# Products with values taken from a queue by pairs of heads in the last attention loop, with other TensorE work in every second round

## The chip, the cores and the metric

The kernel runs on one core of one Trainium2 chip. The metric is the time of the whole kernel on the device, in microseconds; each version is run several times and the median counts. Beside the times there is one profiled execution, whose instructions, waits and transfers can be looked up one by one. TensorE (PE) multiplies matrices, VectorE (DVE) and ScalarE (ACT) work element by element, GpSimd (POOL) does small work and issues stores, and SyncE (SP) issues loads.

## The reference, cut to what matters

Two layers work on 4 images of 64 x 64 positions with 128 channels, so 4096 tokens each. Layer 0 is a selective scan in three directions. Layer 1 is attention with 16 heads of width 8, in which one tensor serves as query, key and value, followed by a small feed-forward part, and then by 64 experts of which each takes its 8 best tokens of an image. What the change touches is the attention of the last image:

```python
qkv = _qz_ring(heads + rx_theta)
q = jnp.transpose(qkv, (0, 2, 1, 3))
scores = jnp.einsum('bhsd,bhtd->bhst', q, q) / np.sqrt(D)
attn = jax.nn.softmax(scores, axis=-1)
ctx = jnp.einsum('bhst,bhtd->bhsd', attn, q)
```

and the gathering of the experts' inputs, which is done on TensorE, with matrices that are zero except at the chosen tokens:

```python
gathered = jnp.take_along_axis(x, flat_idx[:, :, None], axis=1)
pooled = jnp.einsum('bked,bke->bed', gathered, topv)
```

## The kernel before, in words

Attention runs image by image in `loop` (line 948). The loops of the first three images lie beside the scans of the image that follows. This document is about the fourth and last loop, which has no scan left to go with it.

A loop has 1024 **rounds**. A round is one group j of four heads, one block qb of 512 queries and one tile kc of 128 keys; 32 rounds with kc from 0 to 31 make a **turn**. In the last loop the turns are sorted by query block (`by_block`), so that one block of 512 tokens after the other becomes complete, every 128 rounds. A round needs

- `scores` (988): four matmuls on TensorE, two into each of two tiles `s` (PSUM, three of them in rotation), each on a quarter of the array's rows; then two exponentials on ScalarE, each from a tile `s` of 128 x 1024 into a tile `e` (SBUF, pool `a_exps`, four in rotation);
- `values` (1006): four matmuls on TensorE, one for each head of the group, each from half a tile `e` with 32 columns of weights into 32 partitions of the accumulator `acc`. The four lie on four quarters of the array's columns. Heads 0 and 1 read the first tile `e` of the round (pair 0), heads 2 and 3 the second (pair 1).

Within the loop each engine carries out its instructions in the order in which the code issues them: the scheduler is switched to manual. In round i the body of the loop (1040 to 1054) issues the scores of round i + 1, then a share of **other work** (`beside`, 1051), then the values of round i. After a turn `sums` (1018) copies the accumulator to `av` (on VectorE in the last loop), and three rounds later `store` sends `av` to DRAM with five DMAs that GpSimd issues.

The other work of the last loop is a chain of generators, held by `Pace` (1494). Each `yield` ends a step. A step that begins with a matmul is announced by `yield PE`, either by `bank.take` or by `pause` (861), which cuts a group of matmuls in two. `Pace.turn` (1510) adds 1.5 steps of credit in each round and carries out steps while there is credit; a step with a matmul only where the round is `free`, and only one of them in a round. The call at line 1619 says which rounds are free:

```python
block.loop(nb - 1, lambda i: last.turn(1.5, i % 3 > 0 or i > 830), True)
last.rest()
```

So two rounds of three are free up to round 830, and all of them after it. What is not done when the loop ends is carried out by `last.rest()` (1620), before the work that follows. In the chain stand, in this order: `after` for all eight blocks of the third image (context times `w_comb`, norms and the feed-forward part: `first` with matmuls `co`, `second` with matmuls `zt`, `h`, `fo`, `xT`, `lg`), the experts' biases, the search and choice of tokens and the gathering (`pool`, 1333, with four matmuls `wt` and four matmuls `pool` for each of 24 pieces) of images 0 to 2, and then `after` for blocks 0 to 3, 4 to 5 and 6 of the fourth image itself, each of which has to wait until attention has completed its blocks, and one more search. All of these share one PSUM bank (`Bank(…, 1)`), so that a step which wants it waits for the step that has it.

Behind the loop come `closing` (1629), which is `after` for block 7 of the fourth image, the choice and the gathering for that image, the experts, and the scatter of their answers. Weights for three groups of experts are fetched at an early step of `closing` (1632), into memory that the loop has given back.

Of the kernel before, what the change touches and what calls it, by code (L numbers as in the profile page):

```python
# [11 lines left out]
F32 = mybir.dt.float32  # L12
# [4 lines left out]
P = 128  # L17
C = 128
L = 4096
NT = L // P  # L20
# [14 lines left out]
QB = 512  # L35
# [51 lines left out]
PE = "pe"  # L87
# [626 lines left out]
class Attention:  # L714
# [62 lines left out]
    def begin(self, loop):  # L777

        tc = self.tc
        self.pieces_of(loop, 2)  # L780
        self.big = loop.enter_context(tc.tile_pool(name="a_big", bufs=1))
        self.mid = loop.enter_context(tc.tile_pool(name="a_mid", bufs=2))
        self.exps = loop.enter_context(tc.tile_pool(name="a_exps", bufs=4))
        self.ps_s = loop.enter_context(tc.tile_pool(name="a_ps_s", bufs=3, space=PSUM))
        self.ps_o = loop.enter_context(tc.tile_pool(name="a_ps_o", bufs=1, space=PSUM))

# [161 lines left out]
    def loop(self, b, beside, by_block=False):  # L948


        nc = self.nc
        self.cut = by_block
        self.context[b] = self.dram.tile([P, L], F32, name=f"d_ctx_{b}")
        self.total[b] = self.dram.tile([L // QB, H, QB], F32, name=f"d_sum_{b}")
        self.whole[b] = 0
        turns = [(j, qb) for j in range(4) for qb in range(L // QB)]
        if by_block:
            turns.sort(key=lambda turn: turn[1])
        rounds = [(j, qb, kc) for j, qb in turns for kc in range(NT)]
        queries, keys, weights, es, accs, later = {}, {}, {}, {}, {}, {}  # L960
        chunks = [(j, g) for j, _ in turns for g in range(NT // 4)]
        held = {}

        def halves(to, j, cut, first):


            src = self.q[b].rearrange("(k j) x d t -> j k (x d) t", j=4)[j]
            nc.sync.dma_start(out=to, in_=src[:, first * D : (first + 4) * D, cut])

        def fetch(at):  # L970

            if at >= len(chunks):
                return
            j, g = chunks[at]
            if held.get(g) != j:
                held[g] = j
                keys[g] = self.big.tile([P, QB], F32, tag="keys", bufs=10, name=f"key_{b}_{at}")
                halves(keys[g], j, slice(g * QB, (g + 1) * QB), 0)
                weights[g] = self.big.tile([P, 4, VJ], F32, tag="values", bufs=10, name=f"val_{b}_{at}")
                nc.sync.dma_start(out=weights[g], in_=self.v[b][:, j, g * 4 : g * 4 + 4, :])  # L980
            keys[f"{at}"], weights[f"{at}"] = keys[g], weights[g]

        def masked(j, qb):
            t = self.mid.tile([P, QB], F32, tag="qm", name=f"qm_{b}_{j}_{qb}")
            halves(t, j, slice(qb * QB, (qb + 1) * QB), 2)
            queries[j, qb] = t

        def scores(i):

            j, qb, kc = rounds[i]  # L990
            es[i] = []
            cut = slice(kc % 4 * P, kc % 4 * P + P)
            for pair in range(2):
                s_ps = self.ps_s.tile([P, 2, QB], F32, tag="s", name=f"s_{b}_{i}_{pair}")
                for k in range(2):
                    at = 32 * (2 * pair + k)
                    rows = slice(at, at + 32)
                    nc.tensor.matmul(  # L998
                        s_ps[:, k, :], keys[f"{i // 4}"][rows, cut].bitcast(F32R), queries[j, qb][rows, :].bitcast(F32R),
                        start=True, stop=True,  # L1000
                    )
                e = self.exps.tile([P, 2, QB], F32, tag="e", name=f"e_{b}_{i}_{pair}")
                nc.scalar.activation(e, s_ps, AF.Exp, scale=1.0 / math.sqrt(D))  # L1003
                es[i].append(e)

        def values(i):
            j, qb, kc = rounds[i]
            if kc == 0:
                accs[j, qb] = self.ps_o.tile([P, QB], F32, tag="acc", name=f"acc_{b}_{j}_{qb}")
            v = weights[f"{i // 4}"][:, kc % 4, :]  # L1010
            for k in range(4):
                nc.tensor.matmul(  # L1012
                    accs[j, qb][32 * k : 32 * k + 32, :], v[:, k * VW : k * VW + 32],
                    es[i][k // 2][:, k % 2, :], start=(kc == 0), stop=(kc == NT - 1),
                )
            del es[i]

        def sums(j, qb, i):

            av = self.mid.tile([P, QB], F32, tag="av", name=f"av_{b}_{j}_{qb}")  # L1020
            (nc.vector.tensor_copy if by_block else nc.scalar.copy)(av, accs.pop((j, qb)))  # L1021
            cut = slice(qb * QB, (qb + 1) * QB)

            def store():
                for k in range(4):
                    h = 4 * k + j
                    nc.gpsimd.dma_start(  # L1027
                        out=self.context[b][h * D : h * D + D, cut], in_=av[32 * k : 32 * k + D, :]
                    )
                nc.gpsimd.dma_start(  # L1030
                    out=self.total[b][qb].rearrange("(k j) t -> j k t", j=4)[j], in_=av[D::32, :]
                )
                if by_block and j == 3:
                    self.whole[b] = qb + 1

            later[i + 3] = store

        masked(0, 0)
        for at in range(3):
            fetch(at)  # L1040
        scores(0)
        for i, (j, qb, kc) in enumerate(rounds):
            if i % 4 == 0:
                fetch(i // 4 + 3)
            if i + 1 < len(rounds):
                scores(i + 1)
            if kc == NT - 12 and i + 12 < len(rounds):
                masked(*rounds[i + 12][:2])
            if i in later:
                later.pop(i)()  # L1050
            beside(i)
            values(i)
            if kc == NT - 1:
                sums(j, qb, i)
        for i in sorted(later):
            later[i]()
        self.whole[b] = L // QB
# [181 lines left out]
class Experts:  # L1239
# [93 lines left out]
    def pool(self, b, g):  # L1333

        nc, bank, rows = self.nc, self.block.bank, slice(b % 2 * E, b % 2 * E + E)
        x = self.some.tile([P, 4, C], F32, tag="x", bufs=4, name=f"x_{b}_{g}")
        nc.sync.dma_start(out=x, in_=self.block.xn[b][:, g * 4 : g * 4 + 4, :])
        yield
        ps = yield from bank.take(f"wt_{b}_{g}")
        for i in range(4):  # L1340
            at = (g * 4 + i) * P
            nc.tensor.matmul(
                ps[:, i * E : (i + 1) * E], self.chosen[b // 2][rows, at : at + P], self.diagonal[rows, b // 2, :],
                start=True, stop=True,
            )
        yield
        wT = self.some.tile([P, 4, E], F32, tag="wT", name=f"wT_{b}_{g}")
        nc.vector.tensor_copy(wT.rearrange("p i e -> p (i e)"), ps[:, : 4 * E])
        bank.leave()
        yield  # L1350
        ps = yield from bank.take(f"pool_{b}_{g}")
        for i in range(4):
            nc.tensor.matmul(ps[:, :E], x[:, i, :], wT[:, i, :], start=(i == 0), stop=(i == 3))
        yield
        into = self.pooled[:, :, b]
        if g == 0:
            nc.vector.tensor_copy(into, ps[:, :E])
        else:
            nc.vector.tensor_add(into, into, ps[:, :E])
        bank.leave()  # L1360
        yield
# [132 lines left out]
class Pace:  # L1494
# [15 lines left out]
    def turn(self, share, free):  # L1510

        self.credit = min(self.credit + share, 3.0)
        while self.credit >= 1 and not self.done and (free or self.then is not PE):
            free = free and self.then is not PE
            self.step()

    def rest(self):
        while not self.done:
# [3 lines left out]
def tile_kernel(tc, ctx, x, in_proj_w, dirs, out_proj_w, attn, gate, weight1, weight2, out):  # L1522
# [3 lines left out]
    nb = x.shape[0]  # L1526
# [42 lines left out]
    loop = ExitStack()  # L1569
# [39 lines left out]
    with tc.manual_schedule():  # L1609
        last = Pace(  # L1610
            last.parts, experts.biases(),
            *(
                part for images in pairs[:-1]
                for part in (experts.search(images, blocks), experts.choice(images, blocks), experts.gather(images))
            ),
            block.after(nb - 1, range(0, 4)), block.after(nb - 1, range(4, 6)), block.after(nb - 1, range(6, blocks - 1)),
            experts.search(pairs[-1], blocks - 1),
        )
        block.loop(nb - 1, lambda i: last.turn(1.5, i % 3 > 0 or i > 830), True)
        last.rest()  # L1620
        block.cut = False
    loop.close()
# [49 lines left out]
```

## Time and profile before

| what | us |
|---|---|
| median of 3 runs | 11400.93 |
| lowest and highest run | 11396.92, 11414.34 |
| the profiled execution, its own time | 11412.32 |
| the span of its instructions | 11410.5 |
| first exponential of the last loop starts | 9126.4 |
| last product with values of the last loop starts | 11160.8 |
| exponentials in the last loop | 2048 |
| mean granted clock of TensorE over the span | 0.942 |

The profiled execution took 1.8 us more than its span, and 11.4 us more than the median. Times within it are counted from the start of the span. The last loop therefore takes up about 2034 us of it, and what follows about 250 us.

How to read it: the page of a profile gives the busy time of each engine, the busy share in 40 slices of equal length, the chain of work that ended last, and the costliest groups of instructions by line with the mean duration of one and the idle time before them. A timeline lists instructions in order of time and merges equal ones. A table of stretches gives the busy time of each engine between two times, with the granted clock of TensorE.

### The profile page before, as it was taken

The page shows a single profiled execution, that of the slowest core. Times are in us where ns is not written, and L with a number is a line of the kernel's source. Part 1 is how long each engine was busy: PE and PEld are TensorE (multiplying, and loading weights), DVE is VectorE, ACT ScalarE, POOL GpSimd, SP SyncE. Part 2 cuts the span into 40 slices and gives each one's busy share as a digit, 9 for nine tenths or more (in the row PEclk, how much of TensorE's full clock was granted, in tenths as well). Part 3 has the DMA queues.
Part 4 walks back from the last instruction along what each step waited for, and adds up shares of the span by engine and source line. Part 5 has one row for each costly group of instructions (what it writes and reads, how often), then busy time and mean ns, then how long its engine had stood idle before and what let it go on. Part 6 is the DMA issues. An engine that isn't in the chain of part 4 may idle for free.

```text
span 11410.5 us, 183033 instructions
## 1 busy us (share of the span) xinstructions
PE 9874.3 (87%) x68358; PEld 3273.6 (29%) x68358; DVE 8258.3 (72%) x8405; ACT 9993.7 (88%) x10828; POOL 3790.3 (33%) x3891
## 2 busy tenths in 40 slices
PE   6687792788998889899998899999998999999995
PEld 2233331222222222222222222222222223333323
DVE  6889997888888987999988979988998321111212
ACT  4566672899999999999999999999999999989992
POOL 4777784332323223424333124243331110000000
PEclk8798895899999999999999999999999999999997
DMA  6778897656565665665656755656556332222225
GB/s 188 226 231 230 226 249 198 161 145 156 142 155 155 178 174 146 158 154 142 151 147 160 194 157 156 156 141 151 146 147 162 116 100 72 76 71 84 75 65 186
DMA packets 900980, 1747.52 MB, mean 153 GB/s; under 512 B 203150, under 2 KB 443846, under 8 KB 899830
## 3 DMA queue, kind: packets, MB, share of 16 engines
q1 hardware_dynamic: 764734, 1469.68, 47.9%
q0 software_dynamic: 93856, 156.41, 4.8%
q10 hardware_dynamic: 41496, 109.71, 3.6%
q8 instruction: 537, 8.80, 0.3%
q14 instruction: 357, 2.92, 0.1%
HBM read 1379.76 MB, written 355.47 MB: 152 GB/s over the span
## 4 chain that ended last, share of the span: by engine, by line
PE 38%; ACT 24%; issue 14%; DVE 11%; DMA 10%; POOL 1%; SPq 1%; ACTq 0%; DVEq 0%; POOLq 0%
PE acc L1012 21%; ACT e L1003 20%; PE s L998 10%; DVE h L561 5%; DMA delta<-d_delta 4%; PE cv L412 2%; DMA du<-d_du 2%; DVE dB L551 1%; ACT dA L542 1%; PE y L599 1%; ACT delta L542 1%; PE fo L1169 1%; PE xd L426 1%; PE h L1156 1%; DMA w<-in_L_ffn_weight_dram 1%
## 5 line engine op out<-in xcount | busy, mean ns | idle before, releaser
L1003 ACT ACTIVATE e<-s 128x1024 f32<-128x1024 f32 x8192 | 7778.1, 1105 | 234.2 <-PE s L998 222.2
L1012 PE MATMUL acc<-e,val 128*32 128x512 f32 x32768 | 5250.2, 615 | 106.5 <-ACT av L1021 93.7
L998 PE MATMUL s<-qm,key 32*128 32x512 f32 x16384 | 2650.8, 501 | 588.8 <-ACT e L1003 558.9
L998 PEld LDWEIGHTS s<-qm,key 32*128 32x128 f32 x16384 | 1013.4, 184 | 4444.4 <-issue 2483.9
L563 POOL COPY ends<-h 128x1 f32<-128x1 f32 x1152 | 1333.8, 1159 | 2362.4 <-DVE h L561 2353.2
L551 DVE TENSOR_TENSOR dB<-du,B 128x1024 f32<-128x1024 f32 x960 | 1213.6, 1264 | 441.2 <-PE y L599 217.2
L1012 PEld LDWEIGHTS acc<-e,val 128*32 128x32 f32 x32768 | 973.5, 109 | 1608.4 <-issue 789.0
L561 DVE TENSOR_TENSOR_SCAN h<-dA,ends,dB 128x1024 f32<-128x1024 f32 x576 | 1351.2, 2346 | 110.3 <-ACT dA L542 66.2
L542 ACT ACTIVATE dA<-delta,A 128x1024 f32<-128x1024 f32 x768 | 935.7, 1218 | 500.5 <-DMA delta<-d_delta 460.8
L561 DVE TENSOR_TENSOR_SCAN h<-delta,ends,du 128x1024 f32<-128x1024 f32 x432 | 1013.2, 2345 | 127.2 <-ACT delta L542 64.3
L568 POOL TENSOR_TENSOR hC<-h,C 128x1024 f32<-128x1024 f32 x384 | 993.5, 2588 | 153.3 <-PE y L599 83.7
L542 ACT ACTIVATE delta<-delta,A 128x1024 f32<-128x1024 f32 x768 | 937.4, 1221 | 7.3 <-DVE dB L551 2.2
L572 DVE TENSOR_TENSOR du<-h,C 128x1024 f32<-128x1024 f32 x576 | 702.2, 1219 | 0.1
L572 DVE TENSOR_TENSOR dB<-h,C 128x1024 f32<-128x1024 f32 x576 | 702.2, 1219 | 0.0
L551 DVE TENSOR_TENSOR du<-du,B 128x1024 f32<-128x1024 f32 x576 | 691.6, 1201 | 5.8 <-DMA B<-d_bc 5.8
L1027 POOL DMA_DIRECT2D d_ctx<-av x512 | 260.3, 518 | 1026.1 <-DVE av L1021 647.6
L412 PE MATMUL cv<-xn,conv 128*128 128x512 f32 x1024 | 469.7, 612 | 26.8 <-DVE xn L346 17.2
L593 POOL DMA_DIRECT2D d_du<-x_delta x272 | 157.2, 578 | 1003.0 <-DVE x_delta L592 945.1
L561 DVE TENSOR_TENSOR_SCAN h<-dA,dB 128x1024 f32<-128x1024 f32 x192 | 438.9, 2286 | 50.3 <-ACT dA L542 40.9
L599 PE MATMUL y<-hC,sel 128*32 128x256 f32 x3072 | 247.8, 456 | 171.7 <-DVE o L615 160.0
L599 PE MATMUL y<-dB,sel 128*32 128x256 f32 x4608 | 378.8, 401 | 9.9 <-DVE xT L1196 4.8
L561 DVE TENSOR_TENSOR_SCAN h<-delta,du 128x1024 f32<-128x1024 f32 x144 | 329.1, 2285 | 68.3 <-issue 35.0
(246 smaller groups left out, 7200.5 us busy)
## 6 DMA issues: line engine op xcount, KB each, us to landing
delta<-d_delta SPq DMA_DIRECT2D x768, 512.0 KB
du<-d_du SPq DMA_DIRECT2D x576, 512.0 KB
du<-d_du ACTq DMA_DIRECT2D x192, 512.0 KB
key<-d_q SPq DMA_DIRECT2D x352, 256.0 KB
d_u<-u SPq DMA_DIRECT2D x48, 1024.0 KB
d_delta<-r SPq DMA_DIRECT2D x48, 1024.0 KB
B<-d_bc SPq DMA_DIRECT2D x96, 512.0 KB
C<-d_bc SPq DMA_DIRECT2D x96, 512.0 KB
```

The costliest lines, as they stand in the source:

```text
L412: nc.tensor.matmul(banks[2 * m + g], w["conv"][:, k, m * P : (m + 1) * P], reads(k, g), start=(k == 0), stop=(k == 3))
L542: nc.scalar.activation(tiles["delta", s], t, AF.Exp, scale=A)
L551: nc.vector.tensor_mul(tiles["du", s], du, spread[order, c, "B", j % 2])
L561: nc.vector.tensor_tensor_scan(h, dA, dB, first, ALU.mult, ALU.add)
L563: nc.gpsimd.tensor_copy(ends[order, c][:, at : at + 1], h[:, T - 1 :])
L568: nc.gpsimd.tensor_mul(tiles["du", s], h, spread[order, c, "C", j % 2])
L572: nc.vector.tensor_mul(dB, h, spread[order, c, "C", j % 2])
L599: nc.tensor.matmul(y[32 * g : 32 * g + 32, : T // 4], self.sel[:, j // 2, :], hC[:, 256 * g : 256 * g + 256], start=(j == 0), stop=(j == 3),)
L998: nc.tensor.matmul(s_ps[:, k, :], keys[f"{i // 4}"][rows, cut].bitcast(F32R), queries[j, qb][rows, :].bitcast(F32R), start=True, stop=True,)
L1003: nc.scalar.activation(e, s_ps, AF.Exp, scale=1.0 / math.sqrt(D))
L1012: nc.tensor.matmul(accs[j, qb][32 * k : 32 * k + 32, :], v[:, k * VW : k * VW + 32], es[i][k // 2][:, k % 2, :], start=(kc == 0), stop=(kc ...
L1027: nc.gpsimd.dma_start(out=self.context[b][h * D : h * D + D, cut], in_=av[32 * k : 32 * k + D, :])
```

## The change

Six edits, all in effect in the last loop alone, except for the two sizes of buffers.

- `values` is called for one pair of heads at a time. The pairs stand in a queue `due`. In a round in which `turn` tells that a step with a matmul was due (`busy`), the loop takes one pair, and in other rounds up to three; two at most are left standing. The pair that ends a turn also ends the round's share. In the loops of the first three images the queue is emptied in each round, pair 0 and then pair 1.
- `turn` returns whether a step announced as TensorE's was carried out.
- Free rounds are every second one up to round 896 (before: two of three up to round 830).
- In the gathering, the four matmuls `wt` and the four matmuls `pool` are cut in two by `pause`.
- The pool of the tiles `e` has six buffers instead of four.
- `av` has one buffer instead of two.

```diff
-        self.exps = loop.enter_context(tc.tile_pool(name="a_exps", bufs=4))
+        self.exps = loop.enter_context(tc.tile_pool(name="a_exps", bufs=6))
...
-        def values(i):
+        def values(i, pair):
             j, qb, kc = rounds[i]
-            if kc == 0:
+            if kc == 0 and not pair:
                 accs[j, qb] = self.ps_o.tile([P, QB], F32, tag="acc", name=f"acc_{b}_{j}_{qb}")
             v = weights[f"{i // 4}"][:, kc % 4, :]
-            for k in range(4):
+            for k in (2 * pair, 2 * pair + 1):
                 nc.tensor.matmul(
                     accs[j, qb][32 * k : 32 * k + 32, :], v[:, k * VW : k * VW + 32],
-                    es[i][k // 2][:, k % 2, :], start=(kc == 0), stop=(kc == NT - 1),
+                    es[i][pair][:, k % 2, :], start=(kc == 0), stop=(kc == NT - 1),
                 )
-            del es[i]
+            if pair:
+                del es[i]
...
-            av = self.mid.tile([P, QB], F32, tag="av", name=f"av_{b}_{j}_{qb}")
+            av = self.mid.tile([P, QB], F32, tag="av", bufs=1, name=f"av_{b}_{j}_{qb}")
...
-            beside(i)
-            values(i)
-            if kc == NT - 1:
-                sums(j, qb, i)
+            busy = beside(i)
+            due += [(i, 0), (i, 1)]
+            left = 1 if busy and by_block else 3
+            while due and (left > 0 or len(due) > 2 or not by_block or i + 1 == len(rounds)):
+                of, pair = due.pop(0)
+                values(of, pair)
+                left -= 1
+                if pair and rounds[of][2] == NT - 1:
+                    sums(*rounds[of][:2], i)
+                    left = 0
...
         for i in range(4):
+            if i == 2:
+                yield from self.block.pause()
             at = (g * 4 + i) * P
...
         for i in range(4):
+            if i == 2:
+                yield from self.block.pause()
             nc.tensor.matmul(ps[:, :E], x[:, i, :], wT[:, i, :], start=(i == 0), stop=(i == 3))
...
         self.credit = min(self.credit + share, 3.0)
+        busy = False
         while self.credit >= 1 and not self.done and (free or self.then is not PE):
+            busy = busy or self.then is PE
             free = free and self.then is not PE
             self.step()
+        return busy
...
-        block.loop(nb - 1, lambda i: last.turn(1.5, i % 3 > 0 or i > 830), True)
+        block.loop(nb - 1, lambda i: last.turn(1.5, i % 2 > 0 or i > 896), True)
```

More of the change, by code (lines that the diff above doesn't have):

```diff
@@ L959, in loop @@
         rounds = [(j, qb, kc) for j, qb in turns for kc in range(NT)]
-        queries, keys, weights, es, accs, later = {}, {}, {}, {}, {}, {}
+        queries, keys, weights, es, accs, later, due = {}, {}, {}, {}, {}, {}, []
         chunks = [(j, g) for j, _ in turns for g in range(NT // 4)]
@@ L1050, in loop @@
                 later.pop(i)()
-            beside(i)
-            values(i)
-            if kc == NT - 1:
-                sums(j, qb, i)
+            busy = beside(i)
[8 more added lines that the diff above has]
+                    left = 0
+        assert not due
         for i in sorted(later):
```

## The prediction

> **What bounds the kernel now.** I read the page first, for what the last loop (9126 to 11161 us) lives on.
>
> ```profile
> PE   6687792788998889899998899999998999999995
> ACT  4566672899999999999999999999999999989992
> PEclk8798895899999999999999999999999999999997
> L1003 ACT ACTIVATE e<-s 128x1024 f32<-128x1024 f32 x8192 | 7778.1, 1105 | 234.2 <-PE s L998 222.2
> L1012 PE MATMUL acc<-e,val 128*32 128x512 f32 x32768 | 5250.2, 615 | 106.5 <-ACT av L1021 93.7
> ```
>
> From slice 32 on, TensorE and ScalarE are both near full. So the next view is the table of stretches over the loop and what follows.
>
> ```profile
> 9269.00:9808.00 539.00, 535.91 (x3808) 169.16 (x3800) 82.41 (x212) 533.63 (x576) 44.80 (x80) 1.00 0.23 70
> 10000.00:10343.00 343.00, 327.33 (x2322) 122.86 (x2322) 54.27 (x81) 307.79 (x339) 14.23 (x27) 0.98 0.25 70
> 11161.00:11228.00 67.00, 19.88 (x72) 14.35 (x68) 19.33 (x60) 4.36 (x6) 10.93 (x20) 0.60 0.43 145
> ```
>
> Columns: length; busy time of PE, weight loads, DVE, ACT, POOL; clock; DMA. In the first stretch (`second` of image 2) ScalarE is 99% busy; in the second (gathering) 90%; in the third, behind the loop, all engines mostly idle: one block's chain, step after step. Counting exponentials, the first stretch runs at 1.87 us a round, the gathering at 2.05 to 2.3, and the last 64 rounds, without other work, at 1.84. ScalarE alone would need 1024 x 1.84 = 1885 of the loop's 2034 us. At most 149 us can be won there.
>
> Third, the timeline of TensorE, for the price of a round.
>
> ```profile
> 9601.37 0.59 PE L998 MATMUL s<-qm,key 32*128 32x512 f32 x4
> 9601.89 0.71 PE L1169 MATMUL fo<-w,h 128*128 128x128 f32 x4
> 9602.53 1.07 PE L1012 MATMUL acc<-e,val 128*32 128x512 f32 x8
> 9603.53 0.51 PE L998 MATMUL s<-qm,key 32*128 32x512 f32 x4
> ...
> 9605.62 1.05 PE L1012 MATMUL acc<-e,val 128*32 128x512 f32 x4
> ```
>
> Start to start: scores 0.43 us (9603.53 to the values at 9603.97), one cut step `fo` 0.64, all four heads' values 1.00. The last line is decisive. It is from a window that ends at 9606.1, where pair 1 still waits for its exponential: pair 0 is alone (4 records, two passes of fp32 for each head) and spans 1.05 us, against 1.07 for four heads. Its second pass starts 0.455 us after the first, as with four. A pair alone costs TensorE what both together cost.
>
> **What the Trainium skill says.** "TensorE: Matmul & The Clock Gate", section "Measured speedup vs the span model": a packed group spans one matmul's duration plus about 4 ns for each tile, so the number of tiles hardly counts. The trace agrees: heads start 5 to 7 ns apart, and 1.05 stands against 1.07. "TensorEngine Tiling (Array Packing)", section "Key Properties": another tiling mode drains the array. Here 1.00 between values and the next scores is two passes of 0.455 and 0.09 on top; I take the 0.09 as the drain. The first page, Part 1: after about 3.4 us idle the clock halves. The records of the granted clock show 0.5 after each PE gap over 3 us in the loop (at 9825, 9996, 10037, 10239).
>
> **The change, part by part.**
>
> *Values by pairs.* The order of the instructions in both built programs gives the rounds. Before: 409 with other TensorE work, always two pairs. After: 387 with other work (328 with one pair, 59 with two), 99 with one pair although no matmul came (a step announced as TensorE's that found the bank taken), 427 with three pairs, 109 with two. Nearly every busy round in even places is followed by one of three pairs. Of three pairs two lie on the same half of the columns, so they go one after the other: 4 x 0.455 + 0.09 = 1.91 instead of 1.00. The busy round gains nothing, since its lone pair still takes 1.00. So TensorE gets 427 x 0.91 = +389 us.
>
> *Sum of TensorE in the loop.* Scores and values: 1023 x 1.43 = 1463. Other work before: 120 `h` x 0.43, 120 `fo` x 0.64, 30 `co` x 0.64, 30 `zt` x 0.31, 30 `xT` x 0.37, 30 `lg` x 0.57, 48 `wt` and `pool` x 1.03 (each distance read from the timeline as for `fo`; `h` less the 0.09 that the scores before it save) = 235. Sum 1698, or 1.66 a round: below ScalarE's 1.84, which is why ScalarE sets the pace. After: 96, 96, 26, 24, 24, 24 of the first six and 96 halves of `wt` and `pool` at 0.6 (between half of 1.03 and the 0.64 of two `fo`) = 207. Sum 1463 + 389 + 207 = 2059, or 2.04 a round over rounds 64 to 831. TensorE becomes the bound. A round with `fo` and its successor cost 2.07 + 2.34 = 4.41, where ScalarE needs 3.68.
>
> *Stalls.* Before, 21 gaps of TensorE over 1 us in the loop sum to 63 us (context blocks waiting for the shares, `chosen` twice 4.5 us, norms, two table loads for each sine), some 14 us of half clock come on top. About 9 us belong to blocks that leave the loop. 54 + 14 stay, and I add 10 for stretches where ScalarE still leads. Loop after: 2059 + 78 = 2137, +103. Bounds: no stall seen once the pace is slower, 2059 (+25); all stalls and 20 us of new ones, 2175 (+141).
>
> *Free rounds and halves.* With one free round in two and each gathering group taking two steps, the other work falls back. In the order of after, the gathering starts at round 548 instead of 465 and ends at 816 instead of 599; at round 1023 the norms of block 5, `second` of blocks 4 and 5, all of block 6 and the last search are not yet issued. Before, the chain was empty at round 952. They go into `last.rest()`, with no attention beside them, in one PSUM bank. Cost, from rows of the tail of before: `first` behind `co` 7.5 us, cosines 2; in `second`, each of four `h` needs matmul, VectorE 0.75 and two hand-overs, 1.9; each of four `fo` 1.4; norms and adds 11.6 (11213.4 to 11225); `xT` and `lg` 3.5. Blocks 4 and 5 overlap in part: about 73 us from the loop's end, block 7's `co` standing in between. Block 6: shares 10 (load, reciprocal, store, load), `first` 10, cosines 2, `second` to its norms 29. Block 7's `zt` comes about 126 us after the loop's end instead of 36.5: +90. Bounds: two of the blocks overlapping fully, +60; half clock in all of it, +120. Their loads go ahead of block 7's on SyncE, their stores on GpSimd, both inside this sum; the loads of three groups of experts' weights on ScalarE's queue move back too. They landed 100 us before use, so 0 here, up to 15 if they hold up block 7's loads.
>
> *Buffers.* Six `e` instead of four: 0 in the first three loops, where the tile that is overwritten was read before the scores that lead to it were issued (the order of all engines is the same there up to the last loop). One `av`: the copy waits for five stores of the turn before, landed about 6 us after their issue in round 3 of 32: 0, with more than 45 us of cover. Without that cover, the copy and behind it VectorE's queue and the next turn's first product would wait.
>
> *Sum.* 103 + 90 = 193 on the profiled execution's 11412.3: 11605. It stood 11.4 above the median, so 11594 for the median.
>
> **The rivals.**
>
> *Tail only costs* (loop as before or at ScalarE's pace, one pair costs half). If a lone pair took 0.55, a busy round would cost 1.62 and a full one 1.89, ScalarE would stay the bound, and the loop would fall to 1885 + 43 for the stalls that no order hides = 1928: -106. With +90 behind it: 11385, not slower. It decides where a lone pair costs under about 0.6. For it: that is the only reading in which the queue helps. Against it: the 1.05 above.
>
> *The rest overlaps.* If `last.rest()` hid beneath block 7's chain, only the loop would lose: 11504. Against it: one bank, and VectorE's order puts block 7's norm after block 6's.
>
> *Cold clock.* Gaps in the loop over 3 us double and the tail runs at half clock: +141 and +135, 11677.
>
> **How the numbers follow.** Main case 0.70 (11540 to 11650). Rest overlaps or stalls vanish 0.12 (11480 to 11540). Cold 0.10 (11650 to 11700). Cheap pair 0.08, of which half within 0.2% (23 us, what a measurement of this kernel can tell from no change) and half below. The range leaves out the cheap pair and the ends: 11490 to 11690.
>
> **What would show it.** Right: mean round 2.0 to 2.1 us in rounds 64 to 800, ScalarE about 90% busy there and waiting for `s`; three-pair rounds whose values take 1.9; `zt` of blocks 4 to 6 behind the last exponential; the 250 us from the last exponential to the end growing to about 340. Wrong: ScalarE still at 99%, or a lone pair at half the price, or blocks 4 to 6 inside the loop.

## The result: slower by 2.2%

| what | before | after |
|---|---|---|
| median of the runs side by side on one chip, us | 11407.64 | 11667.64 |
| ratio, 95% interval | | 1.0226 [1.0208, 1.0243] |
| span of the profiled execution, us | 11410.5 | 11660.1 |
| last loop: first exponential's start to last exponential's end, us | 2034.4 | 2153.8 |
| tail: from there to the end of the span, us | 249.8 | 382.9 |

By the medians the change costs 260 us. The two spans stand 249.6 apart: +119.4 in the loop, +133.1 in the tail, and -3.0 ahead of the loop. The prediction had +103, +90 and 0.

From the page of after, the lines that answer to those shown of before:

```profile
PE   6687782888998899999998889999989999999984
ACT  4576672999999999999999999999999999989961
L1003 ACT ACTIVATE e<-s 128x1024 f32<-128x1024 f32 x8192 | 7818.4, 1097 | 317.8 <-PE s L998 271.3
L1012 PE MATMUL acc<-e,val 128*32 128x512 f32 x32768 | 5410.3, 613 | 108.4 <-ACT av L1022 93.5
```

The exponentials are no slower one by one (1097 ns), but ScalarE is idle 84 us longer ahead of them (317.8 against 234.2 before), the larger part of it where a tile `s` comes last. The same 32768 products with values keep TensorE busy 160 us longer, although a single one lasts as long as before (613 ns): fewer of them overlap. In the last two slices ScalarE falls to 6 and 1. That is the longer tail.

The table of stretches of after has the columns that the prediction explained. The four stretches are `second` of image 2, the gathering, the tail up to block 7's sine, and a hole that follows it:

```profile
9394.00:9920.00 526.00, 522.68 (x3314) 153.79 (x3312) 63.58 (x165) 485.49 (x512) 38.50 (x69) 1.00 0.20 62
10340.00:10600.00 260.00, 259.72 (x1682) 83.89 (x1679) 10.62 (x27) 240.08 (x252) 10.39 (x20) 1.00 0.23 67
11277.00:11426.00 149.00, 65.42 (x208) 42.59 (x204) 66.68 (x194) 2.19 (x4) 22.32 (x38) 0.56 0.14 43
11426.00:11449.00 23.00, 0.12 (x1) 0.09 (x2) 3.89 (x1) 0.32 (x1) 0.00 (x0) 0.50 1.02 310
```

Two exponentials make a round, so the first stretch has 256 rounds in 526 us and the second 126 in 260: 2.06 us a round in both. TensorE is busy 99% of the time, ScalarE 92%. The bound has changed sides. In the third stretch, most of whose work the loop of before covered, every engine is mostly idle, and TensorE's granted clock is 0.56. In the fourth nothing works for 23 us but DMA, at 310 GB/s.

The timeline of TensorE shows what a round costs now, in two windows (start, duration, engine, line, operation):

```profile
9422.75 1.05 PE L1012 MATMUL acc<-e,val 128*32 128x512 f32 x4
9423.73 0.76 PE L998 MATMUL s<-qm,key 32*128 32x512 f32 x4
9424.42 1.91 PE L1012 MATMUL acc<-e,val 128*32 128x512 f32 x12
...
9601.07 0.50 PE L998 MATMUL s<-qm,key 32*128 32x512 f32 x4
9601.50 1.91 PE L1012 MATMUL acc<-e,val 128*32 128x512 f32 x12
9603.34 0.50 PE L998 MATMUL s<-qm,key 32*128 32x512 f32 x4
9603.67 0.59 PE L1164 MATMUL h<-zT,w 8*128 8x256 f32 x2
9604.19 1.05 PE L1012 MATMUL acc<-e,val 128*32 128x512 f32 x4
9605.18 0.50 PE L998 MATMUL s<-qm,key 32*128 32x512 f32 x4
```

From 9601.07 on: scores 0.43; three pairs (x12) 1.84 from start to start; scores 0.33 and half a group of `h` 0.52; a lone pair (x4) 0.99. Two rounds take 4.11 us, where ScalarE needs 3.68. In the first window a lone pair (0.98) follows a round of three pairs and no other work comes; the scores behind it last 0.69 instead of 0.43, because their second half has to wait until ScalarE has read a tile `s`.

### The profile page after: what moved, and what is told of

Same layout as the page of the kernel before. It is cut to its first block, busy times and chain, and to the rows that moved or that the text cites. A ratio compares the mean times of both kernels' runs of the same rounds, so it can differ in the third digit from the quotient of the medians.

```text
span 11660.1 us, 182497 instructions
## 1 busy us (share of the span) xinstructions
PE 10082.0 (86%) x68358; PEld 3327.9 (29%) x68358; DVE 8256.3 (71%) x8405; ACT 10027.6 (86%) x10824; POOL 3751.8 (32%) x3891
## 4 chain that ended last, share of the span: by engine, by line
PE 38%; ACT 25%; DVE 13%; issue 13%; DMA 10%; SPq 1%; POOL 1%; ACTq 0%; DVEq 0%; POOLq 0%
PE acc L1012 21%; ACT e L1003 20%; PE s L998 9%; DVE h L561 6%; DMA delta<-d_delta 4%; ACT delta L542 2%; PE cv L412 2%; DVE dB L551 2%; DMA du<-d_du 1%; ACT dA L542 1%; PE y L599 1%; PE fo L1177 1%; PE h L1164 1%; DMA w<-in_L_ffn_weight_dram 1%; PE xd L426 1%
## 5 line engine op out<-in xcount | busy, mean ns | idle before, releaser
L1003 ACT ACTIVATE e<-s 128x1024 f32<-128x1024 f32 x8192 | 7818.4, 1097 | 317.8 <-PE s L998 271.3
L1012 PE MATMUL acc<-e,val 128*32 128x512 f32 x32768 | 5410.3, 613 | 108.4 <-ACT av L1022 93.5
L563 POOL COPY ends<-h 128x1 f32<-128x1 f32 x1152 | 1296.0, 1126 | 2380.4 <-DVE h L561 2365.8
L599 PE MATMUL y<-dB,sel 128*32 128x256 f32 x4608 | 376.9, 399 | 10.4 <-DVE xT L1204 4.9
```

The costliest lines, as they stand in the source:

```text
L563: nc.gpsimd.tensor_copy(ends[order, c][:, at : at + 1], h[:, T - 1 :])
L599: nc.tensor.matmul(y[32 * g : 32 * g + 32, : T // 4], self.sel[:, j // 2, :], hC[:, 256 * g : 256 * g + 256], start=(j == 0), stop=(j == 3),)
L1012: nc.tensor.matmul(accs[j, qb][32 * k : 32 * k + 32, :], v[:, k * VW : k * VW + 32], es[i][pair][:, k % 2, :], start=(kc == 0), stop=(kc = ...
```

## The experiments

All of them ran beside the kernel before (medians 11405.93 for the first four, 11412.72 for the others). The loop and the tail are measured in each trace as in the table above:

| kernel | median, us | ratio, 95% interval | loop | tail |
|---|---|---|---|---|
| whole_rounds | 11527.19 | 1.0106 [1.009, 1.0123] | 2016.8 | 383.4 |
| two_pairs_at_most | 11510.52 | 1.0093 [1.0078, 1.0108] | 2000.7 | 382.7 |
| pairs_alone | 11524.86 | 1.0109 [1.0094, 1.0124] | 2152.2 | 248.7 |
| weights_after_sine | 11650.39 | 1.0217 [1.0201, 1.0232] | 2163.6 | 366.7 |
| free_rounds_alone | 11452.49 | 1.0035 [1.0023, 1.0048] | 2034.7 | 281.1 |
| two_pairs_old_free | 11389.34 | 0.9978 [0.9971, 0.9986] | 2010.9 | 250.8 |
| two_pairs_halves | 11371.36 | 0.9968 [0.9956, 0.9981] | 1998.0 | 251.9 |
| two_pairs_halves_weights | 11361.71 | 0.9957 [0.9945, 0.997] | 1998.4 | 239.7 |

The theory: the loop loses by the rounds of three pairs, whose third pair meets the columns of the first, and the tail by the free rounds and halves, which push work behind the loop. The rival: the pairs are harmless, and free rounds, halves or buffers cost all of it.

### Always whole rounds: whole_rounds

After, without the queue's effect; free rounds, halves and buffers stay.

```diff
-            left = 1 if busy and by_block else 3
+            left = 4
```

> The changed kernel with one edit undone: both pairs of a round are issued in their own round, in the order of the kernel before; free rounds, halved gathering and buffers stay. Theory (three pairs in a round put two on the same columns of the array, and that makes TensorE the bound): TensorE's sum falls from 2026 to 1668 us over the loop, ScalarE leads again, the loop takes about 1950 us instead of 2154; the tail stays at 383 us; the whole about 11460. Rival (the spread of the other work over every second round and its stalls slow the loop, not the pairs): the loop stays near 2150, the whole near 11665.

The loop came back by 137 us, and the tail stayed at 383. So the queue as it stands costs the loop 137, and free rounds and halves make the tail. The size was missed by 67 us: the same stretch as above takes

```profile
9394.00:9920.00 526.00, 515.25 (x3574) 154.89 (x3570) 65.63 (x169) 510.47 (x552) 39.15 (x70) 0.98 0.22 66
```

552 exponentials in 526 us, or 1.91 a round, not the 1.85 of ScalarE alone. The expected time had let before's stalls vanish. Charged round by round (the count that the third experiment explains) this loop comes to 1934, and the remainder of 83 is like the 79 of before. In the timeline its values often last longer than 1.07, waiting in the middle for their second tile `e` (this one 1.46), as they do before:

```profile
9600.59 1.46 PE L1012 MATMUL acc<-e,val 128*32 128x512 f32 x8
```

### At most two pairs: two_pairs_at_most

After, with one figure changed: two pairs at most in a round without other TensorE work. Neighbours in the queue lie on different halves of the columns, so of two none waits for the other.

```diff
-            left = 1 if busy and by_block else 3
+            left = 1 if busy and by_block else 2
```

> The changed kernel with at most two pairs in a round instead of three; the queue stays, so pairs still lag by up to a round, and a busy round may still take one pair. Two pairs that follow each other in the queue always lie on different halves of the columns. Theory (same columns twice is the whole cost): no round takes more than 1.0 us for its values, the loop takes about 1950 us, the whole about 11460, like whole rounds. Rival (the lag of the pairs, the queue or the six buffers cost): the loop stays above 2100, the whole above 11610.

The queue, its lag, the six `e` and the one `av` are all still there, and the loop is 153 us shorter than that of after, though some 50 longer than expected. This settles the cause in the loop: not the queue but its third pair. With the third pair the lone pairs go too: in the trace 1021 of the 1024 rounds take exactly two pairs, because otherwise more than two would be left standing. A lone pair that costs as much as two and a third pair that costs extra are one effect seen from two sides, and no run parts them. Four lines of the timeline:

```profile
9605.26 1.06 PE L1012 MATMUL acc<-e,val 128*32 128x512 f32 x8
9606.25 0.91 PE L998 MATMUL s<-qm,key 32*128 32x512 f32 x4
9607.10 1.07 PE L1012 MATMUL acc<-e,val 128*32 128x512 f32 x8
9608.09 0.90 PE L998 MATMUL s<-qm,key 32*128 32x512 f32 x4
```

The values start 1.84 us apart, ScalarE's pace: the values take 1.00 each time, and the scores are stretched to 0.85 because they wait for ScalarE. Against whole_rounds, which differs in nothing but the queue, the loop is 16 us shorter. Since nearly every round takes two pairs, what is left of the queue is a lag: the values come one round later. The waits of the two loops show what it is good for: values wait for their exponentials 389 times in whole_rounds, for 106.7 us, and hardly ever here.

### The pairs alone: pairs_alone

After, with the free rounds of before and without the halves.

```diff
-            if i == 2:
-                yield from self.block.pause()
...
-        block.loop(nb - 1, lambda i: last.turn(1.5, i % 2 > 0 or i > 896), True)
+        block.loop(nb - 1, lambda i: last.turn(1.5, i % 3 > 0 or i > 830), True)
```

> The kernel before with the queue of pairs (one beside TensorE work, up to three otherwise) and the buffers, but its own free rounds (two of three) and the gathering whole. 314 rounds have three pairs instead of 427, and the other work ends in round 952 as in the kernel before. Theory: TensorE's sum 1961 us, between 1.89 and 2.0 a round, a loop of about 2055 us, the tail unchanged at 250: the whole about 11430. Rival (the pairs are harmless and the cost of the change is the work that falls behind the loop): 11408 or less.

```profile
9389.00:9902.00 513.00, 511.93 (x3372) 157.42 (x3368) 77.34 (x203) 482.88 (x513) 42.19 (x75) 1.00 0.22 66
```

The tail is that of before (248.7), the loop that of after (2152.2). The rival falls: the pairs are not harmless. The expected time was missed by 95 us all the same. It rested on TensorE's sum being nearly what the loop takes. With 314 rounds of three pairs that sum is 1961, as expected, well below 2152. The stretch runs at 2.00 us a round, above both TensorE's own sum there (1.94 by the same prices; 1.92 over the whole loop) and ScalarE's 1.84, with TensorE 99.8% busy: stretched scores count as busy. A short round can hardly run ahead, since its scores need a tile `s` that ScalarE has still to read; a long round makes ScalarE wait. If each round is charged the greater of 1.842 and its own sum on TensorE, in the order of the instructions, before comes to 1955 and this kernel to 2090: +135, where +118 was measured.

### The weights' loads behind the sine: weights_after_sine

After, with the three groups of weights asked for at a later step of `closing`, so that the DMA issues on ScalarE's queue come behind block 7's sine.

```diff
-                    if i == 2:
+                    if i == 28:
                         experts.prefetch(room, nc.scalar)
```

> The changed kernel with one move: the loads of three groups of experts' weights are issued on ScalarE's queue after block 7's sine and its four rectified activations instead of ahead of them. Theory (in the changed kernel the sine of block 7 stood 23 us behind these loads, which is the part of the tail that I had set to 0): the tail falls from 383 to about 360 us, the whole to about 11645. Rival (the loads only push the wait elsewhere: the experts then wait for their weights): no change, 11668.

First the hole in after, from the timeline of ScalarE (ACTq is its queue of DMA issues):

```profile
11426.46 0.43 ACTq L1382 DMA_DIRECT2D w<-in_L_ffn_weight_dram  x1
11426.92 2.19 ACTq L1385 DMA_DIRECT2D w<-in_L_ffn_weight_dram  x4
11429.71 0.39 ACTq L1382 DMA_DIRECT2D w<-in_L_ffn_weight_dram  x1
11440.47 2.18 ACTq L1385 DMA_DIRECT2D w<-in_L_ffn_weight_dram  x4
11445.55 0.39 ACTq L1382 DMA_DIRECT2D w<-in_L_ffn_weight_dram  x1
11445.98 2.42 ACTq L1385 DMA_DIRECT2D w<-in_L_ffn_weight_dram  x4
11448.50 0.32 ACT L1234 ACTIVATE z<-z,a_half_pi 128x32 f32<-128x32 f32 x1 [63.70 <-DMA w<-in_L_ffn_weight_dram]
```

VectorE had finished the sine's input at 11425.1. The sine starts 23.4 us later, behind 15 issues, between which the queue stands still for 10.4 and 2.9 us. With the loads behind it:

```profile
11444.31 0.32 ACT L1234 ACTIVATE z<-z,a_half_pi 128x32 f32<-128x32 f32 x1 [40.38 <-DVE z L125]
...
11454.35 0.40 ACTq L1382 DMA_DIRECT2D w<-in_L_ffn_weight_dram  x1
```

Block 7's `zt` stands 148.4 us behind the last exponential instead of 171.6: -23.2, what was expected at that place. Some 7 us of it are lost again on the way to the experts (3.6 of them between `zt` and `xT`), and the tail is 366.7, -16.2. The medians differ by 17, but the intervals of the two ratios overlap, so the reading rests on the trace. The loop, which the edit doesn't reach, was 10 us longer in this execution; that is scatter, and so is no part of the reading.

### The free rounds alone: free_rounds_alone

Before, with the free rounds of after.

```diff
-        block.loop(nb - 1, lambda i: last.turn(1.5, i % 3 > 0 or i > 830), True)
+        block.loop(nb - 1, lambda i: last.turn(1.5, i % 2 > 0 or i > 896), True)
```

> The kernel before with one edit: free rounds are every second one up to round 896; pairs stay together, the gathering is whole, buffers as before. By the order of the instructions only block 6 of the fourth image falls behind the loop (8 of its matmuls h). Theory (the cost of the free rounds is what they push behind the loop): the loop stays near 2030 us, the tail grows by one block's chain of about 58 us plus the wait of block 7's sine behind the weights' loads, to about 330: the whole about 11480. Rival (fewer busy rounds let ScalarE run free, which pays for the block): 11408 or less.

The loop keeps its 2034.7: other work in fewer rounds is neither gain nor loss there. The tail grows by 31, less than the expected 80, since block 6's `first` was still issued inside the loop and its `zt` comes 5.3 us after the last exponential, against 107.6 in after. Even of these 31 us most are not block 6's work but the hole of the experiment before. Block 7's sine, whose input was finished at 11194.4, again stands behind the 15 issues of the weights:

```profile
11218.70 0.32 ACT L1226 ACTIVATE z<-z,a_half_pi 128x32 f32<-128x32 f32 x1 [65.32 <-DMA w<-in_L_ffn_weight_dram]
```

That is 24.3 us of the 33.4 by which block 7's `zt` comes later than before. No run moved the loads in this kernel. The steps that the halves add push the remainder out: of the tail's 133 us about 31 come from the free rounds by themselves, the sine's wait included, and the other 102 only together with the halves.

### A queue that keeps to two pairs: two_pairs_old_free, two_pairs_halves, two_pairs_halves_weights

Before, with the queue, at most two pairs, and the buffers of after; free rounds and gathering as before.

```diff
+            busy = beside(i)
+            due += [(i, 0), (i, 1)]
+            left = 1 if busy and by_block else 2
...
+            av = self.mid.tile([P, QB], F32, tag="av", bufs=1, name=f"av_{b}_{j}_{qb}")
```

> The kernel before with the queue, but at most two pairs in a round, and six buffers e; free rounds and gathering as before, so nothing falls behind the loop. Theory (a lag of pairs lets the values find their exponentials ready, as between whole rounds, 2017 us, and two pairs at most, 2001 us): loop about 2018 instead of 2034, whole about 11392. Rival (the lag gains only where every second round is free): no change, 11406.

```profile
9259.00:9732.00 473.00, 471.90 (x3375) 154.16 (x3371) 77.88 (x204) 471.53 (x512) 41.73 (x74) 1.00 0.23 71
```

256 rounds in 473 us, 1.85 each, with ScalarE 99.7% busy: the loop gets 23 us shorter, and the tail is as before. Here too nearly every round takes two pairs, one round late. How long values wait for their exponentials, in the loop of before and in this one (us in total, times, longest; PEld is TensorE's loading of weights, which comes ahead of each product):

```profile
PEld acc L1012 <- ACT e L1003: 123.1, 424, 0.8
PEld acc L1012 <- ACT e L1003: 2.3, 7, 0.5
```

Next, the gathering in halves, with its free rounds placed so that the tail doesn't grow:

```diff
+            if i == 2:
+                yield from self.block.pause()
...
-        block.loop(nb - 1, lambda i: last.turn(1.5, i % 3 > 0 or i > 830), True)
+        block.loop(nb - 1, lambda i: last.turn(1.5, i % 3 > 0 or i > 680), True)
```

> The same with the gathering in halves and all rounds free from 681 on, so that the other work ends in round 999. Theory (a round costs the greater of ScalarE's 1.84 us and its own sum on TensorE, and gives nothing to the next): 48 rounds with 0.6 us over 1.84 become 96 with 0.17 over it, -13 us: loop about 2005, whole about 11379. Rival (the halves come too late and press on the blocks of the fourth image): 11392 or more.

Another 13 us of the loop, which is what the count by rounds had led to expect, at a tail of 251.9. Last, the weights' loads behind the sine on top of it:

```diff
-                    if i == 2:
+                    if i == 28:
                         experts.prefetch(room, nc.scalar)
```

> The same with the loads of three groups of experts' weights issued after block 7's rectified activations. In the kernel before, block 7's sums and shares stood about 12 us behind these loads. Theory: tail 250 to about 240, whole about 11369. Rival (the experts then wait for their weights, as some of the gain was given back in weights after sine): 11379.

The chain of work that ended last, at the start of the tail of this kernel:

```profile
11129.09 4.40 issue
11133.49 1.75 DMA d_share<-sum
...
11140.11 2.06 PE co L1123 x8
```

Block 7's `co` starts 15.8 us behind the last exponential, against 26.8 in two_pairs_halves, whose chain has 11.55 of issue and 5.48 of `d_share` at this place, for 4.40 and 1.75 here. With the weights' loads moved away, the small store and load of the shares no longer meet them. The tail is 12.2 us shorter. All three medians came within 8 us of what was expected. The gains are small, 0.4% for this last kernel, but the intervals of all three stay below 1.

## Why the prediction held, and where it fell short

The direction, the two places and the mechanism in the loop were right. The forecast of 11594 was 74 us below the median of after. The range held it; the main case's own range (11540 to 11650) did not. The median lies where the prediction had set its cold case (11650 to 11700), so that the range held is in part luck. By the two spans the change was 249.6 us instead of 193: 17 more in the loop, 43 more in the tail, 3 less ahead of the loop. The other 17 of the 74 come from the medians: the profiled execution of before stood 11.4 above its median, that of after 5.8 below its own.

| step of the prediction | predicted | measured |
|---|---|---|
| a lone pair costs what two cost | 1.00 | 0.98 (422 of 427) |
| three pairs | 1.91 | 1.84 (424 of 427) |
| sum of TensorE in the loop | 2059 | 2026 (with these two prices and the halves at 0.59) |
| stalls on top | 78 | 128 |
| loop | 2137 | 2153.8 |
| block 7's `zt` after the loop's end | 126 | 171.6 |
| tail | about 340 | 382.9 |

*Values by pairs.* Right, and shown: two_pairs_at_most, one figure away from after, takes the loop from 2153.8 to 2000.7. The prediction made three pairs four passes of 0.455 and 0.09 of drain. In the trace the passes of such a round start at 0, 0.45, 0.88 and 1.31 us and the next scores at 1.84: the third and the fourth pass follow after 0.43. The next scores start 0.52 us behind the start of the last matmul, with one, two or three pairs alike, so it is the passes that were priced too high and not the drain. That is 30 us too much (427 x 0.07).

*Stalls.* The term that was mis-sized in the loop. The gaps over 1 us came out at 40 us, less than the 54 set down. What was set at "10 for stretches where ScalarE still leads" is 49: 189 times the scores wait for a tile `s` in a round that comes after a short one. Some 38 more (half clock and small waits) are not assigned one by one. The reasoning took TensorE's total as the loop's length, as if a short round could lend all its time to the long one that follows. It lends little: charged round by round, after comes to 2117, which leaves 37, about its gaps. The count is rough, though. It was made after the result, its remainders run from 37 here to 83 in whole_rounds, and it comes out too high in single stretches: 2.08 us a round against the 2.06 of the first stretch above, 1.89 against the 1.85 of two_pairs_old_free. So something of a long round is absorbed. The loop's total was missed by only 17 us because two errors worked against each other: TensorE's sum was set 33 us too high, the stalls 50 too low. And the upper bound of 2175 doesn't follow from its parts: 2059 with all the stalls named (63, 14 and 10) and 20 new ones makes 2166. The waits of after, in the loop, give ScalarE's side of it (us in total, times, longest):

```profile
ACT e L1003 <- PE s L998: 171.3, 444, 7.8
```

Before, the same wait was 99.1 us in 82 times. The 444 are about one for each of the 427 rounds with three pairs. pairs_alone shows the same flaw at greater size, 95 us.

*Free rounds and halves.* The list of what is pushed behind the loop was right: `zt` of blocks 4, 5 and 6 stand 12.2, 28.1 and 107.6 us behind the last exponential. Its prices were low, so low that the tail's +133 lies above the prediction's own bound of +120. From the timeline of TensorE in the tail (in brackets: idle before it, and who ended that):

```profile
11291.25 2.07 PE L1164 MATMUL h<-zT,w 8*128 8x256 f32 x4 [0.83 <-DVE zT L1149]
11294.16 2.07 PE L1164 MATMUL h<-zT,w 8*128 8x256 f32 x4 [0.84 <-DVE h L1167]
...
11343.06 2.07 PE L1177 MATMUL fo<-w,h 128*128 128x128 f32 x8 [0.38 <-DVE x1r L1181]
11345.52 2.07 PE L1177 MATMUL fo<-w,h 128*128 128x128 f32 x8 [0.38 <-DVE x1r L1181]
...
11384.86 1.02 PE L1146 MATMUL zt<-ident,z 128*8 128x128 f32 x4 [8.79 <-ACT z L1234]
...
11448.88 1.02 PE L1146 MATMUL zt<-ident,z 128*8 128x128 f32 x4 [25.80 <-ACT z L1234]
```

A step of `h` mostly takes 2.91 us from start to start, not 1.9, and one of `fo` 2.45, not 1.4. Three blocks with four of each make up about 20 us on the chain, as parts of blocks 4 and 5 overlap. The durations point to the clock: the pauses behind a group are 0.84 and 0.38, while the group itself lasts 2.07. In one bank, each group of matmuls is followed by a hand-over to VectorE, each block by 8 to 12 us for shares and norms, and the mean clock granted is 0.56. The Trainium skill, "TensorE: Matmul & The Clock Gate", section "What's actually happening", gives the full clock after about 3.4 us of sustained work and the half one after about 3.4 us idle. The trace agrees with the fall: full from 11406.9 on, the granted clock is half again from 11410.3, 2.9 us behind the end of the last matmul. The rise comes later and seldom: once among blocks 4 and 5, from 11311.3 to 11318.1, and two of their eight `fo` groups, which lie there, take 1.16 instead of 2.07. That the clock alone makes these 20 us is read from the durations, not tried in a run. The prediction had this in its third rival ("the tail runs at half clock") at 0.10. This half of that rival came true, its other half, doubled gaps in the loop, did not, although its sum of 11677 is the nearest.

*The weights' loads.* "0 here, up to 15" was wrong, and for a wrong reason. The prediction looked at when the weights are used. What counted is what stands behind their issues on ScalarE's queue: block 7's sine, 23.4 us late. weights_after_sine shows it. Where blocks 4 to 6 are done within the loop, the same loads hold up block 7's context instead, and two_pairs_halves_weights shows 12 us for that.

Together: 23.4 and about 20 would make up the 43 us by which the tail's +133 exceeds the predicted +90. The split isn't exact, since moving the loads gave back 16 of the 23.4.

*Buffers, first three loops.* 0, as predicted: the last loop starts 3.0 us earlier, and the kernels with six `e` and one `av` beat before.

*The rivals.* "Tail only costs" needed a lone pair under 0.6; it is 0.98. "The rest overlaps" needed blocks 4 to 6 beneath block 7's chain; block 7's `zt` came after the last of them.

Left open: which waits make up the some 38 us in the loop of after, how much of a long round can be absorbed, and what the tail would take at the full clock. A fourth tile `s`, which might let TensorE run ahead, was not tried.

## What to carry to other kernels

Matmuls that are cut to a part of the array's columns are counted by which columns they take, not by their number: here two of four heads cost as much as four (0.98 against 1.00 us), so a queue of such pieces has to pair pieces on different columns in every round, and one that lets a third in pays for it nearly in full (1.84). What helped in the queue was its lag: with the values one round behind, TensorE no longer waits for exponentials. When two engines meet in every round with few buffers between them, pricing each round by its slower engine comes nearer than pricing the loop by the greater of two sums, if it still leaves some per cent open. Work that was held back in an overlapped loop returned here as a chain with nothing beside it, at a lower clock; and before a step is moved, look at what stands behind its DMA issues on the same engine.

## What the runs showed of the hardware that was not expected

- In a group of products with values on the same columns, the second pass starts 0.45 us behind the first, and each further one 0.43 behind the one before. The next scores start 0.52 us behind the start of the last matmul, whether the group held one, two or three pairs.
- ScalarE's queue can stand still for 10.4 us between two DMA issues (11430.1 to 11440.5) while transfers run at 310 GB/s; an issue itself takes 0.4 to 0.6 us.
- Block 6's groups of `h` and `fo`, with pauses of 0.4 to 0.85 us between them, ran from 11386.7 to 11405.7 at half clock; only the last `fo`, at 1.70 us, was partly faster. With such pauses it took some 20 us until the full clock was granted (11406.9), and the next pause took it away (11410.3). Block 7's `h` and `fo`, one behind the other without such pauses from 11450.7 on, were granted it at 11461.5.
